# Moving W0's low-term stores, two weight loads and r's splits in a fused time-mix and GELU kernel

## The chip, the cores and the metric

The kernel runs on one core of a Trainium2 chip. The metric is the device time of one execution in microseconds (us), given as the median of three runs. Beside these stands one execution that was taken with the hardware profiler; all views of the profile are of that one.

## What is computed

`x` has 4 sequences of 1,024 tokens with 512 channels. It is normalised (`xn`), and two branches of `xn` are added to `x`:

```python
xn = _layernorm(x, axis=-1)
# time mix
xx = jnp.concatenate([xn[:, 1:2, :], xn[:, :-1, :]], axis=1) - xn
k = jnp.einsum('btc,hc->bth', xn + xx * time_mix_k, Wk)
r = jnp.einsum('btc,hc->bth', xn + xx * time_mix_r, Wr)
w = jnp.exp(-jnp.exp(time_decay))
def step(state, kr):
    k_t, r_t = kr
    state = state * w + jax.nn.relu(k_t)
    return (state, state * r_t)
...
out = jnp.einsum('bth,ch->btc', out, Wv)        # then a layer norm with gamma, beta
# feed-forward
D = jnp.dot(xn.astype(jnp.float16).astype(jnp.float32), W0.T) + bias0
D = jax.nn.gelu(D, approximate=False).astype(jnp.float16)
E = (jnp.dot(D.astype(jnp.float32), W1.T) + bias1).astype(jnp.float16)
```

Wk and Wr are 704 x 512, Wv 512 x 704, W0 2,048 x 512, W1 512 x 2,048, all in float32.

## The kernel before

**Blocks and units.** The 4,096 tokens are cut into 8 blocks of 512. A block runs through 16 units, one for each chunk of 128 of W0's 2,048 rows (`NN = 16`). In unit `n` TensorE (PE) does `up` of chunk `n + 2` (W0 times the block, L808, 8 matmuls), `down` of chunk `n` (W1 times the gelu'd chunk, L836, 8 matmuls into four sums) and then a piece of the time mix: `k` and `r` products in units 0 to 11, output products in units 12 to 15. In the first block (`i = 0`) the pieces are raw float32 products (`raw_k`, `raw_r`, `raw_halves`); from the second on they are `three_pass` and `half_pass`, which work on weights split into terms.

**Split weights.** A float32 weight goes to PE as two or three terms. W0 and W1 are split in two, a high and a low one, by `split` (L189): ScalarE (ACT) copies the high term (L190), VectorE (DVE) subtracts it (L191). The high terms of W0 (`w0h`) stay in SBUF for good. The low terms (`w0l`) are used from SBUF in the first block, written to DRAM by `store_w0l` (L207; four DMAs for each group `g` of four chunks, 256 KB each), and from the second block on loaded again chunk by chunk by `load_w0l` (L212), two units ahead of their `up`, into a ring of three buffers. W1's two terms are made in the first block by `load_w1` (L231), written to `w1_dram`, and loaded again afterwards. Wk and Wr are split in three by `split_kr` (L259: `wu`, `wd` and the third term on DVE at L256, L264 and L269, two more on ACT at L267 and L268), written to DRAM, and loaded by `load_kr`. The terms lie in rings of six buffers (`kr`) and two (`w1`); most other tiles of 128 x 512 share 62 slots (`q`).

**Order.** Inside the main loop the order on PE, DVE, ACT and SyncE (SP) is the order in which the program issues the work; these engines run in order. Work off the main path is put into lists: `put(n, fn, ...)` appends to unit `n`, and `woven` (L534) issues it after the unit's matmuls, interleaved with what finishes the last unit's piece. W1's split for chunk `n + 2` is issued behind all of it (L1044, L1045). Stores are collected in `stores` and issued by SP at the end of the unit (`store_weights`). Nearly all DMAs go out on SP, and each of them waits, on one of eight semaphores in turn, for an earlier one to land, so that about eight are under way.

**What the change touches.** `load_w1_raw` (ahead of the loop L862 and in it L1041) asks for W1's chunks. `put(3 + c, load_w0, 3, c)` (L950) asks for W0's last quarter (group 3). The list at L954 says in which unit of the first block which k (`0`) and r (`1`) weight is split; whether a weight is still to be split in the second block is told by `raw_w`, from which `split_kr` takes it (L260, L912, L975). L965 says when each group of W0's low term is stored. `xr_at` (L979), `turns` (L987) and the unit of `split_wv` for Wv's fifth part (L1002) hold for the second block. Ahead of the loop, `first_inputs` keeps PE running with `busy(n)`, products of zeros (L424), around the first transposes (`turned`, L451).

Of the kernel before, what the change touches and what calls it, by code (L numbers as in the profile page):

```python
# [17 lines left out]
P = 128  # L18
# [4 lines left out]
def time_mix_and_gelu_ffn(  # L23
# [36 lines left out]
    NN = N // P  # L60
# [53 lines left out]

    FIRST = 3
    sources = (wkT, wrT)
    raw_w = {}

    def load_raw(kind, h):
        w = part(f"w{'kr'[kind]}_{h}", F32)  # L120
# [89 lines left out]
            stores.append((w0l_dram[g][:, :, c, :].bitcast(F32), terms.bitcast(F32)))  # L210

    def load_w0l(i, n):  # L212
        if i > 0:
            w0ls[i, n] = part(f"w0l_{i}_{n}", tag="w0l", bufs=3)
            g, k = divmod(n, G)
            src = w0l_dram[g][:, k].rearrange("p c k -> p (c k)")
            nc.sync.dma_start(w0ls[i, n].bitcast(F32), src.bitcast(F32))
# [39 lines left out]
        return u  # L257

    def split_kr(block, kind, h, **home):  # L259
        raw = raw_w.pop((kind, h)).rearrange("p c k -> p (c k)")  # L260
        name = f"{kind}_{h}"
        u = truncated(raw, f"wu_{name}")
        d = temp(f"wd_{name}")
        nc.vector.tensor_sub(d, raw, u)  # L264
        home = home or dict(tag="kr", bufs=6)
        terms = [part(f"wt_{name}_{p}", **home) for p in range(3)]
        nc.scalar.copy(terms[0], u)  # L267
        nc.scalar.activation(terms[1], d, AF.Copy, scale=S)  # L268
        nc.vector.scalar_tensor_tensor(terms[2], d, -S, u, ALU.mult, ALU.add)  # L269
        for p in range(3):  # L270
            stores.append((kr_dram[kind, h][p].bitcast(F32), terms[p].bitcast(F32)))
        return [t.rearrange("p (c k) -> p c k", c=NC) for t in terms]
# [138 lines left out]
    def first_inputs(xs, behind):  # L411
# [69 lines left out]
        with tc.manual_schedule(  # L481
            engines={nc.scalar.engine, nc.vector.engine, nc.tensor.engine}
        ):
            nc.scalar.activation(dev[:, 1:2], eps_sb, AF.Sqrt)
            busy(9)
            nc.tensor.transpose(mix_t, mix_rows, ident[: 2 * NC, : 2 * NC])
            first_stats()
            nc.scalar.copy(mix_sb, mix_t)
            nc.scalar.activation(rest_sb, mix_t, AF.Identity, bias=1.0, scale=-1.0)
            busy(1)  # L490
            turned(0)
            busy(2)
            pks = [bank(f"pk_0_{h}") for h in range(FIRST)]
            groups = [(0,), (1,), (2, 3), ()]
            for tiles, following in zip(groups, groups[1:]):
                cols = slice(tiles[0] * P, (tiles[-1] + 1) * P)
                for c in range(NC):
                    if c == NC // 2 + (tiles == (0,)):
                        for s in following:
                            normalized(s)  # L500
                    mixed_first(0, c, cols.start, cols.stop)
                for c in range(NC):
                    if c == NC - len(following):
                        for s in following:
                            turned(s)
                    products(c, cols)
                if tiles == (0,):
                    stats(2)
                    stats(3)
                elif tiles == (1,):  # L510
                    nc.tensor.transpose(late_t, late_rows, ident[: ND + NN, : ND + NN])
            for c in range(NC):
                scaled, added = mixed_first(1, c, 0, TB)
            nc.scalar.copy(late_sb, late_t)
            nc.scalar.activation(w_sb, w_sb, AF.Exp)
            scaled = nc.scalar.activation(w_sb, w_sb, AF.Exp, scale=-1.0)
# [291 lines left out]
    def up(i, n):  # L808
        pd = bank(f"pd_{i}_{n}")
        g, k = divmod(n, G)  # L810
        cols = slice(k * P, (k + 1) * P)
        low = w0ls.pop((i, n)) if i > 0 else None
        for c in range(NC):
            wl = low[:, c * P : (c + 1) * P] if i > 0 else w0l[c, g][:, cols]
            for p, w in enumerate((w0h[c, g][:, cols], wl)):
                nc.tensor.matmul(  # L816
                    pd,
                    w,
                    xf[c],
                    start=(c == 0 and p == 0),  # L820
                    stop=(c == NC - 1 and p == 1),
                )

        def after():
            d16 = const.tile([P, TB], F16, tag="d16", name=f"d16_{i}_{n}")
            nc.scalar.activation(d16, pd, AF.Gelu, bias=b0_sb[:, n : n + 1])  # L826
            if i == LAST and n >= NN - 2:
                d = part(f"d_{i}_{n}")
            else:
                d = part(f"d_{i}_{n}", tag="d", bufs=3)  # L830
            nc.scalar.copy(d, d16)  # L831
            return d

        return after
# [24 lines left out]
    with tc.manual_schedule(engines={nc.sync.engine}):  # L859
        for c in range(NC):  # L860
            load_w0(0, c)
        for n in range(AHEAD + 1):  # L862
            load_w1_raw(n)
        for h in range(FIRST, NF):
            load_raw(0, h)
            load_raw(1, h)
        for kind, src in enumerate(sources):
            nc.sync.dma_start(
                raw_half[:, kind], src.rearrange("(c p) k -> p c k", p=P)[:, :, H0:]
            )  # L870
        for c in range(NC):
            load_w0(1, c)
        x_next = load_x(1, "x")
        for c in range(NC):
            load_w0(2, c)
# [25 lines left out]
    with tc.manual_schedule(engines=engines):  # L901
        for i in range(len(blocks)):
# [6 lines left out]
                bg[n].append(lambda: fn(*args))  # L909

            def fetch_kr(block, kind, h):
                if (kind, h) in raw_w:  # L912
                    ks[block, kind, h] = split_kr(block, kind, h, tag="q", bufs=QS)
                else:
                    ks[block, kind, h] = load_kr(block, kind, h)
# [23 lines left out]
            if i == 0:  # L939
# [7 lines left out]
                put(0, several, split_w0, (1, 2), (1, 3))  # L947
                for c in range(NC):
                    put(2 + c - (c == 0), split_w0, 2, c)
                    put(3 + c, load_w0, 3, c)  # L950
                    put(5 + c, split_w0, 3, c)
                put(1, stats, *range(NS))
                put(3, lambda: norm_apply(j, state["x"]))
                for n, *which in (  # L954
                    (1, 0, 1), (1, 1, 2), (3, 0, 2), (5, 0, 3), (5, 1, 3), (7, 0, 4), (7, 1, 1)
                ):
                    put(n, split_kr, 1, *which)
                put(4, turn, 0, 1)
# [3 lines left out]
                put(9, turn, 11, 16)  # L962
                put(9, load_late_constants)
                put(12, split_half)
                for g, n in enumerate((1, 2, 13, 14)):  # L965
                    put(n, store_w0l, g)
                mix_at = (11, 12, 13, 15)
            else:
                order = [(0, h) for h in range(NF)] + [(1, h) for h in range(NF)]
                for k, (kind, h) in enumerate(order):  # L970
                    if k == NF:
                        for half in range(2):
                            piece(half_at[half], half_pass, i, half)
                    piece(full_at[k], three_pass, i, kind, h)
                    if (kind, h) in raw_w:  # L975
                        put(2, fetch_kr, i, kind, h)
                    elif k > 1:
                        put(full_at[k - 2], fetch_kr, i, kind, h)
                xr_at = {1: (1, 2, 3, 3), LAST: (1, 2, 2, 3)}.get(i, (2, 2, 3, 3))  # L979
                for c, n in enumerate(xr_at):  # L980
                    put(n, split_xr, i, c)
                if j <= LAST:
                    put(1 if i == 1 else 2, fetch_x)
                    for s in range(NS):
                        put(2 + s // 2 if i == 1 else 4, stats, s)
                    put(4 if i == 1 else 5, lambda: norm_apply(j, state["x"]))
                    turns = (2, 4, 4, 4, 2) if i == 1 else (0, 4, 5, 4, 3)  # L987
                    for k in range(sum(turns)):
                        unit = next(n for n in range(5) if k < sum(turns[: n + 1]))
                        put(5 + unit, turn, k, k + 1)  # L990
                mix_at = (10, 12, 13, 14)
            for s, n in enumerate(out_at):
                piece(n, out_piece, i, s)
            put(11 if j <= LAST else 2, fetch_residual)
            if j <= LAST:
                for c in range(NC):
                    put((10, 10, 11, 12)[c], x16, j, c)
                for c, n in enumerate(mix_at):
                    early[n].append((j, c))
                    put(n, mixed, j, c)  # L1000
                    put(n + (n == 10), split_xk, j, c)
                for h, n in {0: WV_FIRST, 1: {NF - 1: 4}}.get(i, {}).items():  # L1002
                    put(n, split_wv, h)
                put(13, fetch_kr, j, 0, 0)
                put(14, fetch_kr, j, 0, 1)

            pe = [ps_e.tile([P, C], F32, tag="pe", name=f"pe_{i}_{s}") for s in range(NS)]
            for n in range(NN):
# [29 lines left out]
                ]  # L1038
                for work, *args in pieces[n]:
                    followers.append(work(*args))  # L1040
                if i == 0 and ahead + 1 < NN:  # L1041
                    load_w1_raw(ahead + 1)
                woven(works, jobs + bg[n])
                if i == 0:  # L1044
                    waiting.append((d, load_w1(*nxt)))  # L1045
# [66 lines left out]
```

## Time and profile before

| | |
|---|---|
| timed runs | 869.02, 871.26, 872.42 us; median 871.26 |
| profiled execution | 869.59 us, span 867.8 us |
| busy: PE, PE's weight loads, DVE, ACT, POOL | 859.3, 691.8, 681.3, 437.1, 79.0 us |
| granted TensorE clock, mean | 0.998 |
| DMA on SP's queue | 200.99 MB, 69.0% of 16 engines |
| HBM read, written | 172.77 MB, 28.84 MB |

The span is the time from the first to the last instruction; the 1.8 us between it and the execution's time lie around it. PE is busy for 99% of the span, so a table of busy times says little about what to change; the questions are where PE isn't at its full rate, and which engine or transfer is just in time there. A busy share is no measure of the rate either: the ends of matmuls are modelled, so rates are read from the starts of matmuls.

In the trace, the second block's first `up` runs at 119 us, before the first block is done at about 140 us, because `up` is two units ahead.

### The profile page before, as it was taken

How to read it: one execution, taken by the hardware profiler on the slowest of the kernel's cores; microseconds unless marked ns; L12 is line 12 of the kernel's file. 1: busy time of each engine (PE TensorE's matmuls, PEld its weight loads, DVE VectorE, ACT ScalarE, POOL GpSimd, SP SyncE). 2: the span in 40 equal slices, each digit the busy share in tenths (PEclk: the TensorE clock that was granted, in tenths of full speed). 3: DMA queues.
4: the chain of work that ended last, by engine and by line, in shares of the span. 5: the costliest groups of instructions: out<-in, count | busy, mean ns of one | idle time of the engine just before them, and what ended most of it. 6: DMA issues, size and time to landing. Idle time of an engine off the chain costs nothing.

```text
span 867.8 us, 11184 instructions
## 1 busy us (share of the span) xinstructions
PE 859.3 (99%) x3750; PEld 691.8 (80%) x3750; DVE 681.3 (79%) x1112; ACT 437.1 (50%) x740; POOL 79.0 (9%) x145
## 2 busy tenths in 40 slices
PE   9998999999999999999999999999999999999998
PEld 8665667788888888888888888888888888888886
DVE  6678898897877978779786888878896887886536
ACT  5846755456534464445635447344563536534422
POOL 1100000000211002000021000100011200200002
PEclk9999999999999999999999999999999999999999
DMA  9789986965578665876559675596666966568634
GB/s 276 266 283 361 335 281 209 338 206 177 178 240 293 211 201 182 267 267 219 176 172 336 209 236 193 183 328 205 210 200 201 321 204 219 185 234 280 201 110 134
DMA packets 104053, 202.36 MB, mean 233 GB/s; under 512 B 11423, under 2 KB 25532, under 8 KB 103996
## 3 DMA queue, kind: packets, MB, share of 16 engines
q1 hardware_dynamic: 103548, 200.99, 69.0%
q8 instruction: 30, 0.49, 0.2%
q10 hardware_dynamic: 448, 0.66, 0.2%
q14 instruction: 27, 0.22, 0.1%
HBM read 172.77 MB, written 28.84 MB: 232 GB/s over the span
## 4 chain that ended last, share of the span: by engine, by line
PE 91%; DVE 3%; DMA 3%; SPq 1%; issue 1%; ACT 1%; ACTq 0%; DVEq 0%
PE pd L816 24%; PE pe L838 24%; PE pa L659 14%; PE oa L756 7%; PE pb L409 7%; PE ob L764 4%; PE ph L688 3%; PE po L715 2%; PE pr L409 2%; DMA w0l<-w0d 2%; PE ob L766 1%; PE pk L409 1%; SPq L225 1%; PE idle L426 1%; DMA w1raw<-in_L_ffn_W 0%
## 5 line engine op out<-in xcount | busy, mean ns | idle before, releaser
L838 PE MATMUL pe<-w,d 128*128 128x512 f32 x1008 | 250.7, 391 | 3.4 <-DVE w L191 2.9
L838 PEld LDWEIGHTS pe<-w,d 128*128 128x128 f32 x1008 | 189.6, 188 | 44.1 <-DVE w L191 3.5
L816 PE MATMUL pd<-xf,w0h 128*128 128x512 f32 x512 | 202.5, 396 | 0.0
L816 PE MATMUL pd<-xf,w0l 128*128 128x512 f32 x512 | 199.7, 390 | 0.3 <-DMA w0l<-w0d 0.2
L826 ACT ACTIVATE d<-pd,late_sb 128x512 f16<-128x512 f32 x128 | 87.7, 685 | 155.3 <-PE pd L816 155.1
L816 PEld LDWEIGHTS pd<-xf,w0h 128*128 128x128 f32 x512 | 96.1, 188 | 23.7 <-issue 2.5
L816 PEld LDWEIGHTS pd<-xf,w0l 128*128 128x128 f32 x512 | 96.1, 188 | 23.0 <-DMA w0l<-w0d 1.5
L672 DVE SCALAR_TENSOR_TENSOR y<-pb,a 128x512 f32<-128x512 f32 x70 | 48.4, 691 | 66.4 <-PE pb L409 65.0
L671 ACT ACTIVATE a<-pa 128x512 f32<-128x512 f32 x70 | 41.9, 598 | 80.6 <-PE pa L659 80.6
L831 ACT CAST d<-d 128x512 fp32r<-128x512 f16 x128 | 79.5, 621 | 4.0
L353 DVE STREAM_TRANSPOSE xnT<-x 32x512 f32<-32x512 f32 x112 | 78.7, 702 | 2.2
L321 POOL TENSOR_SCALAR ry<-mvy 128x1 f32<-128x1 f32 x32 | 18.9, 589 | 427.7 <-DVE mvy L328 427.7
L659 PE MATMUL pa<-hk,kr 128*128 128x512 f32 x140 | 54.5, 389 | 0.0
L659 PE MATMUL pa<-lk,kr 128*128 128x512 f32 x140 | 54.5, 389 | 0.0
L756 PE MATMUL oa<-wv,hg 128*128 128x512 f32 x140 | 54.5, 389 | 0.0
L756 PE MATMUL oa<-wv,lg 128*128 128x512 f32 x140 | 54.5, 389 | 0.0
L659 PE MATMUL pa<-hr,kr 128*128 128x512 f32 x136 | 52.9, 389 | 0.0
L659 PE MATMUL pa<-lr,kr 128*128 128x512 f32 x136 | 52.9, 389 | 0.0
L674 ACT ACTIVATE y<-y 128x512 f32<-128x512 f32 x35 | 22.1, 632 | 43.2 <-DVE y L672 43.2
L771 DVE SCALAR_TENSOR_TENSOR oy<-ob,oa 128x512 f32<-128x512 f32 x28 | 19.4, 692 | 25.2 <-PE ob L766 25.2
L409 PE MATMUL pb<-mk,kr 128*128 128x512 f32 x140 | 37.4, 389 | 0.0
L409 PE MATMUL pb<-mr,kr 128*128 128x512 f32 x136 | 36.3, 389 | 0.0
(166 smaller groups left out, 1341.0 us busy)
## 6 DMA issues: line engine op xcount, KB each, us to landing
w<-w1d SPq DMA_DIRECT2D x110, 512.0 KB, 3.6
kr<-krd SPq DMA_DIRECT2D x207, 256.0 KB, 5.0
w0l<-w0d SPq DMA_DIRECT2D x112, 256.0 KB, 4.1
w1d<-w SPq DMA_DIRECT2D x16, 512.0 KB, 4.6
xres<-in_L_attn_x SPq DMA_DIRECT2D x32, 256.0 KB, 5.6
x<-in_L_attn_x SPq DMA_DIRECT2D x31, 256.0 KB, 5.6
krd<-wt SPq DMA_DIRECT2D x30, 256.0 KB, 4.7
out<-xres SPq DMA_DIRECT2D x28, 256.0 KB, 5.2
```

Of the source, the lines that this page charges most:

```text
L353: nc.vector.transpose(dst[i * Q : (i + 1) * Q, :, :, j, :], src[j * Q : (j + 1) * Q, :, :, i, :],)
L409: return nc.tensor.matmul(dst, w[:, c, :], src, start=(c == 0), stop=(c == NC - 1))
L659: nc.tensor.matmul(pa, w[p][:, c, :], xs[j, c][p], start=(c == 0 and p == 0), stop=(c == NC - 1 and p == 1),)
L671: nc.scalar.activation(a, pa, AF.Copy, scale=1.0 + 1.0 / S)
L672: nc.vector.scalar_tensor_tensor(y, pb, -1.0 / S, a, ALU.mult, ALU.add)
L688: nc.tensor.matmul(pa, w[:, c].rearrange("p two k -> p (two k)"), xs[j, c][p], start=(c == 0 and p == 0), stop=(c == NC - 1 and p == 1),)
L756: nc.tensor.matmul(pa, gs[i, h][p][:, cols], wv[h][p], start=(h == 0 and p == 0), stop=(h == NF - 1 and p == 1),)
L764: nc.tensor.matmul(pb, gs[i, h][2][:, cols], wv[h][2], start=(h == 0), stop=False)
L816: nc.tensor.matmul(pd, w, xf[c], start=(c == 0 and p == 0), stop=(c == NC - 1 and p == 1),)
L826: nc.scalar.activation(d16, pd, AF.Gelu, bias=b0_sb[:, n : n + 1])
L831: nc.scalar.copy(d, d16)
L838: nc.tensor.matmul(pe[s] if sum_ is None else sum_, d[:, s * P : (s + 1) * P], w1[p][:, cols], start=(n == first and p == 0), stop=(n == e ...
```

## The change

- The low term of W0 is no longer stored in units 1, 2, 13 and 14 of the first block, but groups 1 to 3 in its units 12 to 14. Group 0 stays in SBUF for the second block's chunks 0 to 3, which aren't loaded then, and is stored in unit 1 of the second block.
- W1's raw chunks are asked for one unit sooner, and W0's last quarter in units 0 and 1 rather than 3 to 6.
- Of r's weights, part 2 is split in unit 0 rather than 1, and part 3 in unit 1 rather than 5. A set `made` tells which weights are split, so that a raw weight can be split before its raw product has run.
- In the second block the splits of r's inputs go to units 2 to 5 rather than 1 to 3, the transposes of the next block's x to units 6 to 9 rather than 5 to 9, and the split of Wv's fifth part to unit 11 rather than 4. For the other blocks the new `turns` are the old ones written differently.
- One `busy(1)` ahead of the first transposes is left out.

```diff
-    raw_w = {}
+    raw_w, made = {}, set()
...
     def load_w0l(i, n):
-        if i > 0:
+        if i > 1 or i == 1 and n >= G:
...
     def split_kr(block, kind, h, **home):
-        raw = raw_w.pop((kind, h)).rearrange("p c k -> p (c k)")
+        made.add((kind, h))
+        raw = raw_w[kind, h].rearrange("p c k -> p (c k)")
...
             nc.scalar.activation(rest_sb, mix_t, AF.Identity, bias=1.0, scale=-1.0)
-            busy(1)
             turned(0)
             busy(2)
...
-        low = w0ls.pop((i, n)) if i > 0 else None
+        low = w0ls.pop((i, n), None)
         for c in range(NC):
-            wl = low[:, c * P : (c + 1) * P] if i > 0 else w0l[c, g][:, cols]
+            wl = low[:, c * P : (c + 1) * P] if low is not None else w0l[c, g][:, cols]
...
-        for n in range(AHEAD + 1):
+        for n in range(AHEAD + 2):
             load_w1_raw(n)
...
-                if (kind, h) in raw_w:
+                if (kind, h) not in made:
                     ks[block, kind, h] = split_kr(block, kind, h, tag="q", bufs=QS)
...
                     put(2 + c - (c == 0), split_w0, 2, c)
-                    put(3 + c, load_w0, 3, c)
+                    put(c // 2, load_w0, 3, c)
                     put(5 + c, split_w0, 3, c)
...
                 for n, *which in (
-                    (1, 0, 1), (1, 1, 2), (3, 0, 2), (5, 0, 3), (5, 1, 3), (7, 0, 4), (7, 1, 1)
+                    (0, 1, 2), (1, 0, 1), (1, 1, 3), (3, 0, 2), (5, 0, 3), (7, 0, 4), (7, 1, 1)
                 ):
                     put(n, split_kr, 1, *which)
...
-                for g, n in enumerate((1, 2, 13, 14)):
-                    put(n, store_w0l, g)
+                for g in range(1, NN // G):
+                    put(11 + g, store_w0l, g)
...
-                xr_at = {1: (1, 2, 3, 3), LAST: (1, 2, 2, 3)}.get(i, (2, 2, 3, 3))
+                xr_at = {1: (2, 3, 4, 5), LAST: (1, 2, 2, 3)}.get(i, (2, 2, 3, 3))
...
-                    turns = (2, 4, 4, 4, 2) if i == 1 else (0, 4, 5, 4, 3)
+                    turns = (4, 4, 4, 4) if i == 1 else (4, 5, 4, 3)
                     for k in range(sum(turns)):
-                        unit = next(n for n in range(5) if k < sum(turns[: n + 1]))
-                        put(5 + unit, turn, k, k + 1)
+                        unit = next(n for n in range(4) if k < sum(turns[: n + 1]))
+                        put(6 + unit, turn, k, k + 1)
...
+            if i == 1:
+                put(1, store_w0l, 0)
...
-                for h, n in {0: WV_FIRST, 1: {NF - 1: 4}}.get(i, {}).items():
+                for h, n in {0: WV_FIRST, 1: {NF - 1: 11}}.get(i, {}).items():
...
-                if i == 0 and ahead + 1 < NN:
-                    load_w1_raw(ahead + 1)
+                if i == 0 and ahead + 2 < NN:
+                    load_w1_raw(ahead + 2)
```

## The prediction

> **What bounds the kernel now.** I read the page's busy shares first, then the waits of TensorE, then the windows of 10 us, and last the timelines of the stretches that the windows single out. PE is busy for 99% of the span, so only its own stalls can be won back, and only new stalls can be lost.
>
> The list of TensorE's waits (engine, line, waited for; total us, times, longest) has five rows, of which these matter:
>
> ```profile
> PE pe L838 <- DVE w L191: 2.9, 2, 2.7
> ...
> PE pe L838 <- ACT w L190: 0.5, 1, 0.5
> ...
> PE pd L816 <- DMA w0l<-w0d: 0.2, 1, 0.2
> ```
>
> The windows place them (PE busy, its weight loads, DVE, ACT, POOL, each with a count, then granted clock, DMA share, GB/s):
>
> ```profile
> 70.00:80.00 10.00, 7.35 (x26) 5.45 (x25) 9.79 (x15) 7.44 (x13) 0.56 (x1) 0.87 1.02 364
> 80.00:90.00 10.00, 10.00 (x36) 6.73 (x35) 9.68 (x16) 6.00 (x10) 0.00 (x0) 0.96 0.93 327
> ...
> 150.00:160.00 10.00, 10.00 (x46) 8.29 (x45) 7.20 (x13) 5.16 (x9) 0.00 (x0) 1.00 0.97 318
> 160.00:170.00 10.00, 9.68 (x42) 7.40 (x41) 9.09 (x16) 4.47 (x8) 1.27 (x2) 1.00 1.00 366
> ```
>
> At 70 to 80 us DVE is full, PE loses 2.65 us, and the granted clock drops; at 140 to 172 us the DMA engines are full, and PE waits a little for W0's low term. PE's timeline gives the two stalls of the first block:
>
> ```profile
> 51.47 0.50 PE L838 MATMUL pe<-w,d 128*128 128x512 f32 x1 [0.49 <-ACT w L190]
> ...
> 76.84 2.92 PE L838 MATMUL pe<-w,d 128*128 128x512 f32 x7 [2.65 <-DVE w L191]
> ```
>
> I price a stall by starts. One chunk without a block-0 piece takes 3.63 us (47.19 to 50.82), one with a raw product 7.14 us (62.85 to 69.99). Chunk 3's `down` is due at 50.82 and chunk 4's then at 57.96; it came at 59.22, so 1.26 us are lost there. Chunk 7's is due at 73.62 and chunk 8's at 80.76; it came at 85.47: **4.7 us lost**, 2.65 idle, the rest mostly the half-rate clock that the trace records for 3.41 us from 77.4 on (1.7 us). In the second block units of 6.35 us (144.46 to 150.81 to 157.15) run late by 0.4 and 0.5 us at low-term chunks 6 and 7.
>
> **The change, part by part.** The sum is made against the profiled execution's 869.59 us; the three timed runs have a median of 871.26, 1.67 higher, and I carry the difference over to that median.
>
> *Start, -0.3 (0 to -0.4).* One warming product, which waited 0.34 us for `rest_sb`, goes from ahead of the first transposes. These then wait for DVE's normalised columns, which end at 5.98, against the transposes' end at 6.92; PE is a closed chain from 7.98 to 31.2, so what is won there stays.
>
> *Sooner loads, 0 by themselves.* W1 runs one chunk further ahead, and W0's last quarter is asked for in units 0 and 1. Three more loads of 256 KB stand on SP's queue ahead of the first stores. The DMA engines lie idle from 34 to 38.6 us, where SP waits for ACT's first split (38.64), so they fit. They end the waits of ACT for W1 (5.2 us in four times in the list of waits), which matter only through the stall at chunk 7.
>
> *r's third split moved from unit 1 to unit 0, and r's fourth from unit 5 to unit 1: +2.5 at chunk 3 (2.0 to 3.0).* This is DVE's timeline of before in that stretch:
>
> ```profile
> 40.73 1.29 DVE L191 TENSOR_TENSOR w0l<-w0raw,w0h 128x512 fp32r<-128x512 f32 x2 [5.13 <-ACT w0h L190]
> 41.94 0.68 DVE L191 TENSOR_TENSOR w<-w1raw,w 128x512 fp32r<-128x512 f32 x1
> 43.52 0.69 DVE L191 TENSOR_TENSOR w0l<-w0raw,w0h 128x512 fp32r<-128x512 f32 x1 [0.90 <-ACT w0h L190]
> ...
> 50.28 0.69 DVE L269 SCALAR_TENSOR_TENSOR wt<-wd,wu 128x512 fp32r<-128x512 f32 x1
> 51.45 0.69 DVE L191 TENSOR_TENSOR w<-w1raw,w 128x512 fp32r<-128x512 f32 x1 [0.48 <-ACT w L190]
> ```
>
> From 43.52 to 50.97 DVE has no gap, and chunk 3's W1 split comes last in it. The built order puts the moved split behind `w0l_3_1` and ahead of chunk 2's W1 split, on both engines. DVE then does `wu` at 41.94, `wd` 42.36 to 43.05, `wt` to 43.78 (0.4, 0.69, 0.69 us). ACT can't do its second term before 43.07, so its W1 copy goes from 41.12 to 43.6, gelu and cast behind it, and `w0h_0_2` from 42.88 to 45.38. DVE's gapless run starts at 46.0 instead of 43.52: all of it is 2.5 us later, since unit 1 gets as much (r's fourth split) as it gave. Chunk 3's W1 terms come at 53.9 and 54.6, and PE, due at 50.8, idles about 3.1 us before the first product. The cover of before, 5.13 us of DVE idle ahead of 40.73, lies on the wrong side: the split is queued behind it. The moved split needs the `kr` buffers of the first one, whose stores leave at 38.64; such stores landed in 2.0 to 2.8 us there, so no wait adds.
>
> *The stall at chunk 7 goes: -4.7 (-4.7 to -2.7).* Unit 5 has 1.78 us less on DVE and no wait for W1: its two waits of 1.06 and 2.60 us behind ACT shrink. With everything 2.5 us later I get chunk 7's W1 at about 73.9, needed at 76.1. Next late is chunk 9's: DVE hands it over at about 86.6, needed at 86.9, so the cover is thin, 0.3 us.
>
> *W0's low term.* Stores of group 1 take the place of four loads and of the old stores of groups 0 and 1: in units 12 to 14, 3 MB of stores against 2 MB of stores and 1 MB of loads, followed by idle DMA from 134 to 140. Nothing there. **Group 0's four stores, though, now stand on SP's queue in the second block's unit 1, between x's loads and the loads of W1 chunk 4 and of low-term chunk 6.** The chain of waits of before says what these are worth (start, us):
>
> ```profile
> 155.34 6.81 DMA w0l<-w0d
> 162.16 6.83 DMA w0l<-w0d
> ```
>
> Low-term chunk 6 lands at 162.16, just when PE wants it. Four stores cost SP 4 x 0.71 = 2.9 us (median issue of `w0d` in the answer on that tensor) and the 16 engines 4 x 512 packets of 512 B x 27 ns / 16 = 3.5 us (median of the packet records; 2,048 B take 84). The Trainium skill (DMA: Bandwidth & Descriptors, Specifications) counts 512 B as enough for line rate; by it the four would cost 4 x 128 x 84 / 16 = 2.7 us. The row decides: 3.5. The stretch is saturated to 172, so nearly all is paid: chunk 6 lands at about 165, +2.9, chunk 7 another +0.4, **+3.3 in sum**. Bounds: 0, if the DMA engines find the room, to 5, if chunk 7's load, which is issued only when 6 has landed, is late in full again.
>
> *The clock, +1.7 twice (0 to 3.4).* Both new stalls are 3.1 to 3.3 us long. The Trainium skill (TensorE: Matmul & The Clock Gate, "Why this matters for your kernels" and Part 1) lets the clock fall after a whole idle window of about 3.4 us that runs freely; by that rule neither stall would do, and the sum would be +0.8. The row: 2.65 us idle was enough. Idles of 0.5 us weren't. I follow the row, with some 0.8 for each.
>
> *r's inputs, transposes and Wv's fifth split later in the second block: 0.* `half_pass` of r runs at 178; its last split is then due from DVE at about 173. Wv's split (1.8 us) pushes g's last split to about 216; its product comes at 217.2. If that cover fails it costs up to 1.3.
>
> **Sum:** -0.3 + 2.5 - 4.7 + 3.3 + 3.4 = **+4.2 us**, 873.8 for the profiled execution, **875.5** on the scale of the median.
>
> **The rivals.**
>
> *One half-rate window less, or two* (chance 0.15): +2.5 or +0.8, 873.8 or 872.1. For it: the free-running window may cut a stall in two; against it, 2.65 us in the row.
>
> *The group-0 stores are hidden* (0.09): -0.3 + 2.5 - 4.7 + 1.7 = -0.8, 870.5. For it: the DMA share is only 0.86 to 0.94 at 156 to 162; against it, the load of chunk 6 lies behind the stores on SP's own queue.
>
> *The other side* (0.12): DVE's run isn't the limit at chunk 3, because the sooner loads let ACT and DVE use their idle time; all block-0 stalls go: -0.3 - 4.7 - 1.3 = -6.3, **865.0**, and up to 868 with part of the store's price. It decides if chunk 3's W1 is split by 50.8 all the same. The order on both engines speaks against it.
>
> *Worse* (0.20): low-term loads stay late chunk after chunk (+5), and chunk 9's thin cover goes (+0.7, with the loss at chunk 7 partly kept): +2 to +4 beyond the forecast, 877.5 to 879.5.
>
> Forecast 0.44, its own range 873 to 878. A change within 0.5% (4.4 us, about what a measurement of this kernel can tell from none) reaches to 875.6, so the forecast's own case lies on its edge: I put 0.26 of its 0.44 beyond, since the thin cover at chunk 9 and at Wv's split can only add, and all of the worse case. Slower 0.46, faster 0.12 (the other side), within 0.42 (the rest). Range: 867 to 880.
>
> **What would show it.** Right: PE idle about 3 us ahead of `down` of chunk 3, near 51 to 54 us, with a half-rate stretch behind; none near 74; PE waiting for `w0l` near 162 for about 3 us; four issues of `w0d` behind x's loads. Wrong: PE's waits on W1 gone altogether, or no wait on `w0l` over 1 us in the second block.

## The result and the profile after

The changed kernel takes **874.55 us** (median of 13 runs, 872.74 to 876.40) against 870.24 us (13 runs, 868.49 to 872.42) of the kernel before in the same comparison: ratio 1.0049, 95% interval 1.0038 to 1.0060. It is slower by 4.3 us, half a per cent. Its profiled execution took 874.51 us, span 872.7, against 869.59 and 867.8: +4.9. PE's busy share is 99% in both.

The list of TensorE's waits of the changed kernel, with the same columns as for the kernel before:

```profile
PE pd L816 <- DMA w0l<-w0d: 4.1, 1, 4.1
PE pe L838 <- ACT w L190: 3.1, 1, 3.1
```

Two waits are new in size, and the wait of 2.7 us on VectorE's W1 split is gone. The windows say where they lie:

```profile
50.00:60.00 10.00, 6.95 (x19) 4.22 (x18) 7.88 (x14) 6.95 (x12) 2.15 (x3) 0.83 0.84 306
...
70.00:80.00 10.00, 10.00 (x40) 7.21 (x39) 8.13 (x13) 6.43 (x11) 0.57 (x1) 1.00 0.60 209
...
160.00:170.00 10.00, 5.85 (x17) 4.35 (x16) 8.98 (x17) 3.21 (x7) 1.27 (x2) 0.67 1.02 346
```

From 70 to 80 us PE now runs without a gap at full clock, and VectorE is busy for 8.13 us there instead of 9.79. The losses have moved to 50 to 60 and to 160 to 170 us, and in both the granted clock falls (0.83 and 0.67) beside the idle time. PE's timeline shows the two places, one in each block:

```profile
54.25 3.79 PE L838 MATMUL pe<-w,d 128*128 128x512 f32 x8 [3.06 <-ACT w L190]
...
165.30 0.79 PE L816 MATMUL pd<-xf,w0l 128*128 128x512 f32 x1 [4.15 <-DMA w0l<-w0d]
```

The eight products at 54.25 take 3.79 us; at full clock eight such products take 1.98.

To compare runs I read the starts of `down` and take the pitch of a stretch without waits off: 10.70 us for two chunks of the first block (in the changed kernel 63.14 to 73.84), 6.35 us for one unit of the second. What is over is lost there, idle time and half-rate time together. The columns are: start of chunk 2's `down`; loss from chunk 2 to 4, from 4 to 6 and from 6 to 8 of the first block; loss from chunk 3 to 5 of the second block, where `up` needs low-term chunks 6 and 7; span. From chunk 8 to the second block's chunk 3, 71.67 to 71.74 us pass in every run but one, and from its chunk 5 to the end 696.8 to 697.2, so these columns hold all that differs.

| kernel | start | 2 to 4 | 4 to 6 | 6 to 8 | low term | span |
|---|---|---|---|---|---|---|
| before | 47.19 | 1.33 | 0.07 | 4.78 | 0.90 | 867.8 |
| changed | 47.41 | 5.03 | 0 | 0 | 6.71 | 872.7 |
| difference | +0.22 | +3.70 | -0.07 | -4.78 | +5.81 | +4.9 |
| changed, r's splits as before | 46.50 | 1.29 | 0 | 0 | 6.24 | 867.3 |
| changed, group 0 stored in unit 7 | 47.42 | 5.08 | 0 | 0 | 1.73 | 867.6 |
| changed, group 0 stored from ACT | 46.05 | 6.46 | 0 | 0 | 7.71 | 873.8 |
| changed, PE kept busy | 46.31 | 3.86 | 0 | 0 | 5.22 | 868.9 |
| changed, splits spread, stored in unit 7 | 47.41 | 0 | 0 | 1.24 | 3.79 | 865.8 |
| before, no `busy(1)` | 46.58 | 1.33 | 0.25 | 5.98 | 2.79 | 870.3 |
| before, loads only | 47.66 | 1.29 | 0 | 4.55 | 0.90 | 867.7 |
| before, splits spread | 46.34 | 0 | 1.75 | 1.34 | 4.16 | 868.3 |
| before, stores only | 46.04 | 1.29 | 0 | 0 | 1.18 | 862.1 |
| before, stores and loads | 47.22 | 1.33 | 0 | 0 | 2.89 | 864.8 |
| before, stores, x later | 46.57 | 1.26 | 0 | 0.01 | 0 | 861.4 |

The rows below the difference are the experiments. The exception after chunk 8 is the run with the splits spread in the kernel before: it loses another 1.07 us after chunk 8.

The first loss comes as VectorE's timeline of the changed kernel says:

```profile
40.94 1.29 DVE L191 TENSOR_TENSOR w0l<-w0raw,w0h 128x512 fp32r<-128x512 f32 x2 [5.17 <-ACT w0h L190]
...
44.55 0.69 DVE L191 TENSOR_TENSOR w<-w1raw,w 128x512 fp32r<-128x512 f32 x1 [0.53 <-ACT w L190]
46.31 0.69 DVE L191 TENSOR_TENSOR w0l<-w0raw,w0h 128x512 fp32r<-128x512 f32 x1 [1.06 <-ACT w0h L190]
...
54.23 0.69 DVE L191 TENSOR_TENSOR w<-w1raw,w 128x512 fp32r<-128x512 f32 x1 [0.48 <-ACT w L190]
```

Before, the three later rows stood at 41.94, 43.52 and 51.45. All of unit 1's work is 2.6 to 2.8 us later, because r's moved split sits ahead of it, and the 5.17 us of idle time stay where they were, ahead of the split. The second loss is on SP's queue, in the second block:

```profile
153.28 1.76 SPq L111 DMA_DIRECT2D x<-in_L_attn_x  x4
155.09 3.30 SPq L225 DMA_DIRECT2D w0d<-w0l  x4
158.49 1.31 SPq L242 DMA_DIRECT2D w<-w1d  x1
159.84 0.45 SPq L217 DMA_DIRECT2D w0l<-w0d  x1
```

The load of low-term chunk 6 is issued last, after x and the four stores of group 0, and lands 5.41 us later; PE has wanted it since 161.15.

### The profile page after: what moved, and what is told of

It is laid out like the page before. It is cut to its first block, busy times and chain, and to the rows that moved or that the text cites. A ratio compares the mean times of both kernels' runs of the same rounds, so it can differ in the third digit from the quotient of the medians.

```text
span 872.7 us, 11171 instructions
## 1 busy us (share of the span) xinstructions
PE 860.6 (99%) x3748; PEld 693.7 (79%) x3748; DVE 680.6 (78%) x1112; ACT 437.7 (50%) x740; POOL 78.0 (9%) x145
## 4 chain that ended last, share of the span: by engine, by line
PE 96%; DVE 1%; DMA 1%; ACT 1%; issue 0%; ACTq 0%
PE pd L816 26%; PE pe L838 26%; PE pa L659 15%; PE oa L756 7%; PE pb L410 7%; PE ob L764 4%; PE ph L688 3%; PE pr L410 2%; PE po L715 2%; PE pk L410 2%; PE ob L766 1%; DMA w0l<-w0d 1%; PE pkr L633 0%; DMA x<-in_L_attn_x 0%; PE pt L454 0%
```

## The experiments

Each ratio is to the kernel before on the same chip in the same comparison (medians 870.04, 869.90 and 870.10 us in the three comparisons).

**r's splits put back** in the changed kernel: does the split order cost what chunk 3 loses?

```diff
-                    (0, 1, 2), (1, 0, 1), (1, 1, 3), (3, 0, 2), (5, 0, 3), (7, 0, 4), (7, 1, 1)
+                    (1, 0, 1), (1, 1, 2), (3, 0, 2), (5, 0, 3), (5, 1, 3), (7, 0, 4), (7, 1, 1)
```

> The changed kernel with r's third and fourth splits back in units 1 and 5. Theory (two separate costs, the moved split at chunk 3 and the group-0 store in the second block, against one gain at chunk 7): chunk 3's idle falls from 3.06 to about 0.5 us and its half-rate stretch goes; chunk 7 idles at most 0.5 us, because the sooner W1 loads alone end ACT's waits there; the wait for w0l at chunk 6 of the second block stays at 3 to 4 us. Sum against before: -4.4 + 5.8 = +1.4 us, some 871.7. Rival (chunk 7's gain comes from r's fourth split leaving unit 5): 2 us or more of idle come back at chunk 7, with a half-rate stretch: some 875.

Measured: 869.94 us, ratio 1.0001 (0.9992 to 1.0010); each set against its own kernel before, that is 4.4 us below the changed kernel, and below both expectations. Chunk 3's loss is 1.29 again, so the moved splits made it. But chunk 7 lost nothing either, with r's two splits back in unit 5, where I had looked for its cause. The low-term loss stayed at 6.24.

**Group 0 stored in unit 7** of the second block instead of unit 1:

```diff
-                put(1, store_w0l, 0)
+                put(7, store_w0l, 0)
```

> The changed kernel with group 0 of W0's low term stored in unit 7 of the second block instead of unit 1. Theory (these four stores delay low-term chunk 6): the wait of 4.1 us near 161 us goes but for about 0.4, and so do its two half-rate windows; the rest as in the changed kernel: 5.8 us less than it, some 868.7. Rival (that stretch is short of DMA time anyway, and the stores only add a little): a wait of 1.5 us or more stays, some 871 to 873.

Measured: 870.01 us, ratio 0.9997 (0.9987 to 1.0007), 4.3 us below the changed kernel in the same way. It lies between the two expectations: the low-term loss falls from 6.71 to 1.73, and a wait of 1.1 us stays. SP's queue and PE's timeline of this run:

```profile
155.51 0.43 SPq L217 DMA_DIRECT2D w0l<-w0d  x1
```

```profile
162.28 0.50 PE L816 MATMUL pd<-xf,w0l 128*128 128x512 f32 x1 [1.09 <-DMA w0l<-w0d]
```

The load is issued 4.33 us sooner and is there 3.0 us sooner (PE goes on at 162.28 instead of 165.30, both after the same chunk at 156.2): the four stores delay it by 3.0.

**Group 0 stored from ScalarE's queue**, still in unit 1: is it SP's order or the bytes?

```diff
+    def store_w0l_act(g):
...
+            nc.scalar.dma_start(
+                w0l_dram[g][:, :, c, :].bitcast(F32), terms.bitcast(F32)
+            )
...
-                put(1, store_w0l, 0)
+                put(1, store_w0l_act, 0)
```

> The changed kernel with group 0's four stores in unit 1 of the second block issued from ScalarE's queue instead of SyncE's. Order theory (the low term of chunk 6 comes late because its load stands behind x, the stores and a W1 load on SyncE's queue): the load is issued some 3.3 us sooner, near 156.5, so the wait before the low-term chunk near 161 falls from 4.1 us to about 1 us, no half-rate stretch follows, and the time is about 870 (-4.5 us against the changed kernel). Rival, bandwidth (the bytes of the stores and of x delay the load wherever they are issued): the wait stays at 2.5 us or more and the time at 873 or above.

Measured: 874.27 us, ratio 1.0041 (1.0026 to 1.0055): nothing won. SP's queue no longer carries the stores, yet the chain of waits of this run (start, us) reads:

```profile
148.38 8.70 DMA w0d<-w0l
157.08 0.02 issue
157.09 0.33 SPq L111
...
157.94 7.85 DMA w0l<-w0d
```

The load of chunk 6 left 1.9 us sooner than in the changed kernel (157.94 against 159.84), but took 7.85 us instead of 5.41, and PE still waited 4.2 us. The last store took 8.70 us to land, and x's last load was held until it had. So another queue didn't help. The run doesn't separate the bytes from that hold of x cleanly; it rules out that SP's order of issue alone costs the 3 us.

**`busy(1)` left out of the kernel before:**

```diff
-            busy(1)
```

> The kernel before, without the one warming product. The prediction's step: 0.3 us sooner at the first up (31.2 us in the kernel before). Rival, from the changed kernel's trace, where the transposes begin 0.5 us sooner and the first products' run is longer by as much: no gain, 0 to +0.2 us. Both some 870; the trace decides by the start of the first up.

Measured: 869.93 us, ratio 1.0003 (0.9991 to 1.0014). No gain. In its profiled execution the first `up` starts at 30.02 us instead of 30.64, but the run with the stores alone, whose code is the same up to there as in the kernel before, starts it at 29.45. Kernels with the same code up to chunk 0 of the first block (before, splits spread, stores only) start its `down` at 36.49, 35.64 and 35.34, and the same differences are left in the column of starts. The start varies by over 1 us from execution to execution, so a gain of 0.3 can't be seen.

**The sooner loads alone** in the kernel before:

```diff
-        for n in range(AHEAD + 1):
+        for n in range(AHEAD + 2):
...
-                    put(3 + c, load_w0, 3, c)
+                    put(c // 2, load_w0, 3, c)
...
-                if i == 0 and ahead + 1 < NN:
-                    load_w1_raw(ahead + 1)
+                if i == 0 and ahead + 2 < NN:
+                    load_w1_raw(ahead + 2)
```

> The kernel before, with only the sooner loads (W1 one chunk further ahead, W0's last quarter asked for in units 0 and 1). Theory: chunk 7's stall of 2.65 us shrinks to 0.5 or less and its half-rate stretch goes: some 4.4 us less than before, 866. Rival (the stall is DVE's own work in unit 5, the loads only moved transfers): 2 us or more of idle stay, some 869 to 870.

Measured: 869.45 us, ratio 0.9995 (0.9986 to 1.0003). My theory fell: chunk 7 still loses 4.55. ScalarE's timeline of the kernel before and of this run have the same row at the same time:

```profile
65.90 0.62 ACT L190 CAST w<-w1raw 128x512 fp32r<-128x512 f32 x1 [3.29 <-DMA w1raw<-in_L_ffn_W]
```

```profile
60.63 0.62 ACT L190 CAST w<-w1raw 128x512 fp32r<-128x512 f32 x1 [0.46 <-DMA w1d<-w]
...
65.97 0.62 ACT L190 CAST w<-w1raw 128x512 fp32r<-128x512 f32 x1 [2.96 <-PE pe L838]
```

The last row of each is the split of W1's chunk 6. The raw data are there sooner, and ScalarE now waits as long for something else: the ring of two W1 buffers, which is free when chunk 4's terms have been used and stored. The row names PE, but the products of chunk 4 had ended at 61.6, before the wait began at 63.0. What was left is the store; the split of chunk 5, at 60.63, waits for such a store by name, though the landing of chunk 4's own isn't in the trace. That store stood on this run's SP queue behind eight stores of W0's low term:

```profile
52.62 3.18 SPq L225 DMA_DIRECT2D w0d<-w0l  x4
55.91 0.79 SPq L225 DMA_DIRECT2D w1d<-w  x1
...
57.50 3.57 SPq L225 DMA_DIRECT2D w0d<-w0l  x4
61.17 0.92 SPq L225 DMA_DIRECT2D w1d<-w  x1
```

From this comes the next theory: what frees chunk 7 is that the eight stores leave units 1 and 2.

**The stores alone**, moved in the kernel before to the late units:

```diff
-                for g, n in enumerate((1, 2, 13, 14)):
+                for g, n in enumerate((11, 12, 13, 14)):
```

> The kernel before with the stores of W0's low-term groups 0 and 1 moved from units 1 and 2 to units 11 and 12 of the first block, nothing else: W1's chunks and W0's last quarter are loaded when they were. Theory (the eight stores ahead of W1's stores and loads on SyncE's queue are what makes W1 late for chunk 7): chunk 7's wait falls from 2.5 us to under 1 us and its half-rate stretch goes; the time falls by about 4 us to 866, unless the low-term chunks of the second block take it back. Rival (the sooner loads are needed as well): chunk 7 still waits 1.5 us or more, 869 to 870.

Measured: **865.40 us**, ratio 0.9946 (0.9932 to 0.9960). Chunk 7 loses nothing. SP's queue of the kernel before, then SP's queue and ScalarE's timeline of this run:

```profile
56.60 3.55 SPq L225 DMA_DIRECT2D w0d<-w0l  x4
60.25 1.21 SPq L225 DMA_DIRECT2D w1d<-w  x1
61.51 0.92 SPq L229 DMA_DIRECT2D w1raw<-in_L_ffn_W  x1
```

```profile
53.27 0.32 SPq L225 DMA_DIRECT2D w1d<-w  x1
54.02 0.33 SPq L229 DMA_DIRECT2D w1raw<-in_L_ffn_W  x1
```

```profile
60.73 0.61 ACT L190 CAST w<-w1raw 128x512 fp32r<-128x512 f32 x1
```

Chunk 4's store and chunk 6's raw load leave at 53.27 and 54.02 instead of 60.25 and 61.51, and the split of chunk 6 runs at 60.73 without a wait. From chunk 2's start that is 14.7 us instead of 18.7. The raw load takes about as long to land as before (4.0 us, 4.3 before), so what the stores cost is the time at which it leaves.

**The splits alone**, spread in the kernel before, stores and loads left alone:

```diff
-                    (1, 0, 1), (1, 1, 2), (3, 0, 2), (5, 0, 3), (5, 1, 3), (7, 0, 4), (7, 1, 1)
+                    (1, 0, 1), (2, 1, 2), (3, 0, 2), (4, 1, 3), (5, 0, 3), (7, 0, 4), (7, 1, 1)
```

> The kernel before with r's splits spread over units 1, 2, 3, 4, 5, 7, 7, its stores and loads left alone. Theory (chunk 7's 2.5 us belong to the stores of units 1 and 2, not to VectorE's splits in unit 5): chunk 7 still waits about 2.5 us and is followed by a half-rate stretch; at most 1.3 us of the small stalls of chunk 3 go: 869 to 870. Rival (r's two splits in unit 5 hold W1's chunk 7 up): chunk 7's stall and its stretch go, about 866.

Measured: 868.29 us, ratio 0.9984 (0.9974 to 0.9994), and neither expectation held. Chunk 3 loses nothing, and chunk 7's wait shrinks, but a new one stands ahead of it, in PE's timeline:

```profile
68.35 0.49 PE L816 MATMUL pd<-xf,w0h 128*128 128x512 f32 x1 [0.90 <-ACT w0h L190]
...
74.55 1.88 PE L838 MATMUL pe<-w,d 128*128 128x512 f32 x7 [1.01 <-DVE w L191]
```

Chunks 4 to 8 and what follows lose 1.75 + 1.34 + 1.07 = 4.2 us instead of 4.85. Where the lateness comes out thus depends on where VectorE's splits stand. Not all of it is the stores': with this list chunk 7 loses 1.24 us in the next run too, where they stand late.

**Both faults of the change mended:** the changed kernel with the spread list and with group 0 stored in unit 7 (the two edits above).

> The changed kernel with r's splits spread over units 1, 2, 3, 4, 5, 7, 7 (half, so that no unit before 7 has more than one) and group 0's stores moved to unit 7 of the second block. Theory (both stalls of the change are put back, and chunk 7's stall of before is gone with the stores out of units 1 and 2): the first block runs without a wait over 1 us, the low-term chunk 6 waits 0 to 2 us; about 865 (ratio 0.994). Rival (the low-term chunk's wait brings its half-rate stretch all the same, some 4 us): 869 to 870, no different from before.

Measured: 866.02 us, ratio 0.9950 (0.9937 to 0.9963). The direction is right, the size 1 us short: chunk 7 loses 1.24 (PE waits 0.90 us there for VectorE's W1 split), and the low-term chunk waited 1.9 us, with a half-rate stretch.

**PE kept at work through the two waits** of the changed kernel, by products whose sums the real ones overwrite:

```diff
+        for _ in range({(0, 5): 13, (1, 6): 17}.get((i, n), 0)):
+            nc.tensor.matmul(pd, w0h[0, g][:, cols], xf[0], start=True, stop=True)
```

> The changed kernel with TensorE kept at work through its two waits: 13 extra products (0.227 us each, 2.95 us) ahead of the first block's product of chunk 5, which stands just before the 3.06 us wait, and 17 (3.86 us) ahead of the second block's product of chunk 6, which waits 4.15 us. Their sums are overwritten by the real products. Clock theory: both waits fall under 0.5 us, the half-rate stretches after them do not come, the path loses the 1.7 to 5.1 us that the clock cost and gains nothing else: 869.5 to 873 median, granted clock 0.998 or more. Rival (the half-rate stretch costs nothing of its own, since the products it slows would have waited anyway): no half-rate stretch, and 874 to 875.5 all the same. If the work that the waits are for is itself held up by the extra products, the time rises by up to 6.8 us, their own length.

Measured: 870.86 us, ratio 1.0013 (1.0007 to 1.0020). PE's timeline of this run:

```profile
53.89 1.88 PE L840 MATMUL pe<-w,d 128*128 128x512 f32 x7 [0.22 <-DVE w L191]
...
158.47 4.02 PE L814 MATMUL pd<-xf,w0h 128*128 128x512 f32 x17
...
163.00 0.50 PE L818 MATMUL pd<-xf,w0l 128*128 128x512 f32 x1 [0.29 <-DMA w0l<-w0d]
```

No work was taken away, and 30 products were added, but PE is no longer idle for over 0.5 us at these places, and its clock records show no half-rate stretch there (mean 0.999 against 0.994). The losses fall from 5.03 to 3.86 and from 6.71 to 5.22: **the half rate itself cost 1.17 and 1.49 us** on the path. The medians put the gain at 3.5 us (4.3 above the kernel before, now 0.8); the start, 1.1 us sooner in this execution, may be part of that.

**The stores and the loads** together in the kernel before (the two edits above):

> The kernel before with the stores of groups 0 and 1 moved to units 11 and 12 and with W0's last quarter and W1 loaded as soon as in the changed kernel; r's splits, the kept group and the rest as before. Theory (the stores alone free chunk 7, the sooner loads add nothing): the same as the stores alone, 865 to 866. Rival (the sooner loads take the last 0.5 us wait for W1 in the first block away): 864.5. Other rival (a W1 chunk loaded sooner finds no buffer, or delays the stores of k's terms): above 866.5.

Measured: 864.79 us, ratio 0.9952 (0.9938 to 0.9966); the interval overlaps that of the stores alone. The sooner loads add nothing that can be measured, and the half microsecond that PE waits for W1 at chunk 3 stays (loss 1.33).

**The stores, and x's load a unit later** in the second block of the kernel before:

```diff
-                    put(1 if i == 1 else 2, fetch_x)
+                    put(2, fetch_x)
...
-                        put(2 + s // 2 if i == 1 else 4, stats, s)
-                    put(4 if i == 1 else 5, lambda: norm_apply(j, state["x"]))
+                        put(4, stats, s)
+                    put(5, lambda: norm_apply(j, state["x"]))
```

> The kernel before with the stores of W0's low-term groups 0 and 1 moved to units 11 and 12, as in the run of the stores alone (865.4), and in the second block x's load for the next block in unit 2 instead of 1, its statistics in unit 4 and its normalization in unit 5. Theory (what is left is the low-term chunk 6's load behind x's 1.05 MB): the wait of 0 to 2 us at that chunk goes and none comes in its place: 864 to 865. Rival (chunk 7's low term then comes behind x, whose wait takes the place of chunk 6's): 865.5 to 868.

Measured: **864.50 us**, ratio 0.9937 (0.9925 to 0.9949), the lowest of all. Its interval overlaps that of the stores alone, so 0.9 us between the two isn't shown by the medians. The profile shows what it does, on SP's queue:

```profile
147.67 0.42 SPq L217 DMA_DIRECT2D w0l<-w0d  x1
...
150.39 2.57 SPq L111 DMA_DIRECT2D x<-in_L_attn_x  x4
```

Chunk 6's load leaves before x, and the low term costs nothing. The five runs lie within 1.3 us (863.32 to 864.63); those of the stores alone spread over 4.0 us (863.96 to 868.00). What varies in the other kernels would then be this wait: in profiled executions of kernels with the same code around it, it was 0.2, 0.6, 2.2 and 2.4 us. That is argued from a few executions, not shown.

## Why the prediction was right

The predicted time was 875.5 us, the measured one 874.55; the sum in the profiled execution was +4.2, measured +4.9. The two losses came where and for the reasons that were given; the gain came for another reason, and that its size fitted is luck. The errors of the terms also cancel in part: +0.5 at the start, -0.5 at chunk 3, -0.15 at chunks 4 to 8, +0.8 at the low term. Taken by its terms:

- **Start, -0.3 predicted, +0.22 measured: wrong.** The transposes did begin 0.5 us sooner (5.57 instead of 6.07), but the first products took as much longer. The effect, if there is one, is below the start's own variation of over 1 us.
- **Chunk 3, +2.5 and 1.7 of clock predicted, +3.70 measured: right.** Place, cause and size. Without the half rate the loss is 3.86 - 1.33 = 2.5 us, the predicted term; the half rate cost 1.17 instead of 1.7. VectorE's run was predicted to start at 46.0 and started at 46.31.
- **Chunk 7, -4.7 predicted, -4.78 measured: right in size, wrong in its cause.** The step said that unit 5 "has 1.78 us less on DVE and no wait for W1". With r's split back in unit 5 the stall is gone all the same, and with the loads alone it stays. It is the low term's stores, which left units 1 and 2; moving them alone takes the stall away. What the moved split would have done without them wasn't run in the changed kernel. The prediction costed those stores where they went, units 12 to 14, and not where they came from, in front of W1's stores and loads on SP's queue; the lines of that queue, with 3.00 and 3.55 us of `w0d` ahead of W1's, were in the trace of before.
- **Low-term chunks 6 and 7, +3.3 and 1.7 of clock predicted, +5.81 measured: right, 0.8 short.** The stores delay chunk 6 by 3.0 us (predicted 2.9; between the 2.7 and the 3.5 us that the step worked out for the DMA engines). Without the half rate the loss is 5.22 - 0.90 = 4.3 us, 1.0 over the term. Chunk 7 isn't the reason: in the run with PE kept at work it adds 0.79 us against 0.49 before, 0.3 of the 0.4 that I allowed it. The 1.0 us stands at chunk 6 and isn't the stores': with them in unit 7, chunk 6 still loses 1.38 us against 0.41 before. In both kernels x's first load leaves later beside PE's work than before, 2.95 (changed) and 3.04 us (stored in unit 7) ahead of chunk 3's `down` instead of 4.09, since it waits 3.1 us instead of 1.5 for a store of `out` to land. That this makes up the 1.0 us is argued, and what holds `out` up stays open.
- **The clock, 3.4 predicted, 1.17 + 1.49 = 2.7 measured.** The choice that the text had to make was between the Trainium skill's window (TensorE: Matmul & The Clock Gate, Part 1, an idle window of about 3.4 us), by which neither stall as predicted would slow the clock, and the row of 2.65 us that did. The row was right: 3.06 us slowed it. The stall of 4.15 us did too, but it is longer than that window and doesn't decide. (The page's section "Why this matters for your kernels", which the step names as well, puts the limit at gaps over some 3 us; 3.06 is at its edge, 2.65 below it.) Counting half of a 3.41 us stretch as lost was right for the products: the eight at 54.25 take 3.63 us from start to start instead of 1.82. But at full clock PE would have waited there for VectorE's W1 split, as in the run with PE kept at work, where the same eight take 2.45 us. So 1.17 of it is lost on the path. After the 4.15 us wait the trace shows two stretches (6.83 us from 163.39 on), 1.9 us of which fell into the wait; and the rest covered a wait of 0.50 us for chunk 7 that PE has in the run at full clock.
- **At nothing:** chunk 9, r's inputs, the transposes and Wv's split in the second block. The stretches after chunk 8 and after the second block's chunk 5 are as long as before to 0.04 us, so these covers held.

The rival that all block-0 stalls go (865.0) failed at chunk 3, as the order on both engines said. But its time is about that of a version that leaves r's splits alone and only moves the stores: the gain of chunk 7 was there to be had without the two losses.

## What to carry to other kernels

A moved DMA has two ends: price what its queue does once it is gone from the old place as well as what it delays at the new one. Here eight stores of 3 to 3.6 us per group stood ahead of the stores that free a ring of two buffers, and moving them alone was worth 0.5%. When a wait goes and the next instruction starts no sooner, look at what that instruction waits for next: the loads alone changed the name of the wait, not its end.

Do one part of a bundle alone before believing in the whole; of this one, a part won 4.8 us and two others lost 9.5. Where an idle gap can't be removed, products that are thrown away can keep the clock up through it.

## What the hardware showed

- In these runs every idle gap of PE of 2.4 us or more inside the two blocks was followed by the half rate, and none of 1.7 us or less (stores and loads) was. In between the length doesn't tell: 1.9 us of idle PE brought a stretch of 3.41 us once (both faults mended), 2.2 us once none (the run without `busy(1)`, at its low-term chunk). Stretches came as 3.41 us or twice that, after equal gaps too: 2.65 us at chunk 7 brought one in the kernel before and two in the run without `busy(1)`, and 3.06 us at chunk 3 one in the changed kernel and two in the run with stores from ScalarE's queue, where the loss is 6.46 us instead of 5.03.
- One of four stores moved to another engine's queue took 8.70 us to land beside SP's traffic and held up a load on SP's queue until then.
